# Layer one's bases of an R-GCN with the partition as (row, basis) and rows eight apart

## The chip, the core and the metric

The kernel runs on one core of one Trainium2 chip. The time is that of one execution on the device, in microseconds, as the median of several runs. A profiled execution is a separate run; its own device time and its span (first to last instruction) stand beside the median below.

## What is computed

Two blocks of a graph network over 625 nodes with 512 features. Each has a graph part, a linear attention and a mixture of experts. The change lies in the first graph part, a relational graph convolution with two relations, whose weights are mixed from 30 bases:

```python
def rgcn_gate_layer(x, row, col, edge_type, basis, att, gate_w, root, bias):
    w = jnp.einsum('rb,bio->rio', att, basis)      # basis (30, 512, 512), att (2, 30)
    x_j = x[col]
    msgs = []
    for r in range(2):
        gate = jax.nn.sigmoid(x_j @ gate_w[r, :, 0])
        msgs.append(gate[:, None] * x_j @ w[r])
    msg = jnp.where((edge_type == 0)[:, None], msgs[0], msgs[1])
    agg = jax.ops.segment_sum(msg, row, num_segments=x.shape[0])
    return agg + x @ root + bias

h = jax.nn.relu(rgcn_gate_layer(x, row, col, edge_type, basis1, att1, gate_w1, root1, bias1))
out = rgcn_gate_layer(h, row, col, edge_type, basis2, att2, gate_w2, root2, bias2)
```

Inputs and output are float32. The first line of the function is what matters here: for layer one, 30 x 512 rows of 2 KB, 31.5 MB, are read from HBM and summed into w[0] and w[1], 512 rows each.

## The kernel before

**Mixing layer one's bases** (`mix_bases_1`, lines 311 to 343) is done on PE in 32 steps q. A step takes 32 rows i of the weight (4 groups j of 8 neighbouring rows) and one half of the bases (15 of 30, g = q % 2). Its tile `basis` has 120 partitions, one for each pair (basis, row within the group), and four blocks j of 512 columns. Line 325 fills it with four loads on SP's queue, each of 15 bases x 8 rows x 512 values. Step q multiplies each block with `att1`, a matrix of 120 x 32 that holds att[r, b] where the partition's row is the column's row, and zero elsewhere (line 334). So 32 rows of PSUM get, in their first 16, the mixed rows (row, relation) of the group j; the second half of the bases is accumulated on the first. After every second step ACT copies the four groups to a tile `stage` (line 338), and POOL issues four small writes (line 341), each of which moves 16 rows of `stage` to 8 partitions of `wmix`, the weights as the messages need them: row i at partition i % 128 and column block i // 128.

`att1` is made once at the start (lines 436 to 452): `att_pick` repeats columns of the identity so that a matmul (line 444) brings att to the 120 partitions, `att_mask` (line 446) has a one where the partition's row is the column, and line 450 multiplies them.

**What runs beside it.** The stage that lasts until 185 us builds the matrix of edge counts: fifteen groups (`count_group`, lines 219 to 236) of one-hot rows made by DVE and ACT and multiplied on PE. Between groups, the loop of lines 536 to 552 places one or two mixing steps (`mix`), a piece of the linear attention, three or two additions of the first slice of layer two's weights (`slice0`, DVE, line 367) and the loads for it on POOL's queue (`ring`, line 356). The weights `wk`, `wv`, `wq` are loaded on SP's queue between the basis loads. The order of PE and SP is written out by hand here (`manual_schedule`), so both work through these calls in the order of the code. The tiles `basis` come from a pool with three buffers: a load waits until PE has used the tile before the last two.

**The last four steps** are threaded between layer two's other slices (`slices`, 30 loads of 768 KB into the same pool, added on DVE) in the order "DPDPDPDP" and then only D, lines 568 to 594, three loads ahead. Then `messages` (line 627) reads `wmix`: its first matmul needs every write of line 341.

Of the kernel before, what the change touches and what calls it, by code (L numbers as in the profile page):

```python
# [14 lines left out]
OP = mybir.AluOpType  # L15
AX = mybir.AxisListType
# [5 lines left out]
D = 512  # L22
# [4 lines left out]
NB = 30  # L27
BGROUPS = (15, 15)
BROWS = 8
# [16 lines left out]
def kernel(ctx: ExitStack, tc: tile.TileContext, A, out: bass.AP):  # L46
    nc = tc.nc
# [11 lines left out]
    ident = const.tile([128, 128], F32, name="ident")  # L59
# [111 lines left out]
    def one_bank():  # L171
        return banks[1].tile([128, BANK], F32, name="ps1")

    def mix_bank():
        return banks[2]()
# [135 lines left out]
    def mix_bases_1(wpool):  # L311

        w = wpool.tile([128, 2, KD * D], F32, name="wmix")
        src = A["L0_gnn_basis1"].rearrange("b (i c) o -> i b c o", c=BROWS)
        acc = [None]

        def loaded(q):  # L320
            i0, g = 4 * (q // 2), q % 2
            n, b0 = BGROUPS[g], sum(BGROUPS[:g])
            bt = basis_pool.tile([128, KD, D], F32, name="basis")
            for j in range(4):
                nc.sync.dma_start(bt[:BROWS * n, j, :], src[i0 + j, b0:b0 + n])
            return bt

        def step(q, bt):
            i0, g = 4 * (q // 2), q % 2
            k = BROWS * BGROUPS[g]  # L330
            if g == 0:
                acc[0] = mix_bank()
            for j in range(4):
                nc.tensor.matmul(acc[0][32 * j:32 * j + 32, :], att1[g][:k], bt[:k, j, :],  # L334
                                 start=(g == 0), stop=(g == 1))
            if g == 1:
                sg = stage_pool.tile([128, D], F32, name="stage")
                nc.scalar.copy(sg, acc[0])  # L338
                for j in range(4):
                    k, p0 = (i0 + j) // 16, 8 * ((i0 + j) % 16)  # L340
                    nc.gpsimd.dma_start(w[p0:p0 + 8, :, k * D:(k + 1) * D], sg[32 * j:32 * j + 16, :])  # L341

        return w, [(lambda q=q: loaded(q), lambda bt, q=q: step(q, bt)) for q in range(32)]

    class Added:
# [91 lines left out]
    b0 = 0  # L437
    for n in BGROUPS:
        k = BROWS * n
        pick = dec.tile([NB, 128], F32, tag="part", name="att_pick", bufs=3)  # L440
        nc.vector.tensor_copy(pick[:, :k].rearrange("p (b c) -> p b c", b=n),
                              ident[:NB, b0:b0 + n, None].to_broadcast([NB, n, BROWS]))
        ps = one_bank()
        nc.tensor.matmul(ps[:k, :2], pick[:, :k], attT, start=True, stop=True)
        mask = rowsA.tile([128, BROWS], F32, name="att_mask", bufs=2)
        nc.vector.tensor_reduce(mask[:k], ident[:k, :k].rearrange("p (b c) -> p c b", b=n), AX.X, OP.add)
        a = rowsA.tile([128, 32], F32, name=f"att1_{b0}")
        nc.gpsimd.memset(a, 0.0)
        for r in range(2):
            nc.vector.tensor_scalar_mul(a[:k, r:2 * BROWS:2], mask[:k], ps[:k, r:r + 1])  # L450
        att1.append(a)
        b0 += n
# [6 lines left out]
    for i in range(2):  # L459
        g = rowsA.tile([128, KD, 32], F32, name=f"gwp{i}")  # L460
# [46 lines left out]
    def gates_of(psg):  # L507
        gate = rowsA.tile([P, NT, 2], F32, name="gate")
        nc.scalar.activation(gate.rearrange("p t r -> p (t r)"), psg[:P, :2 * NT], AF.Sigmoid)
        return gate  # L510

    wm1, steps = mix_bases_1(wpool)

    def mix(n=1):
# [261 lines left out]
    pick = lpool.tile([P, NT], F32, name="pick")  # L776
# [804 lines left out]
```

## Time and profile before

| | us |
|---|---|
| median of 3 runs | 978.2 (977.06 to 979.41) |
| the profiled execution, device time | 975.78 |
| its span | 974.0 |
| PE busy | 890.9 (91%) |
| DVE busy | 514.2 (53%) |
| ACT busy | 304.1 (31%) |
| POOL busy | 142.8 (15%) |
| basis loads of line 325: first and last issue | 3.3 and 215.4 |
| one issue of line 325 on SP's queue (median of 128) | 0.838 |
| one mixing matmul of line 334 (256 in all), mean of the first 224, median of the last 32 | 0.650, 0.617 |
| writes of line 341: one issue on POOL, median landing | 0.550, 6.7 |

The profile divides the span into 40 equal slices and gives busy shares in tenths (a 9 is 90% or more), the clock granted to PE in tenths, and for the DMA engines the mean busy share of sixteen and the rate:

```profile
PE   3898899979999999789969999999988899997997
DVE  7778694566889723422254632233355754566320
PEclk9999999999999999799989999999999999997999
DMA  8899997575487920889831111212210104020001
GB/s 243 244 280 259 251 248 185 169 196 196 135 285 230 334 87 2 265 292 331 281 120 56 44 43 47 81 46 87 86 64 27 61 1 128 10 77 2 0 6 47
```

Each slice is 24.4 us. The count stage takes the first seven and a half. PE is busy nearly everywhere; the DMA engines are busy in the first half of the span and mostly idle in the second. A group of instructions is listed by line, engine, operation, output and inputs; "mean ns" is one instruction, and the idle time is that of its engine just before.

### The profile page before, as it was taken

Reading aid. Unit: us, or ns where it says so; the run is one execution under the profiler, and the core shown is the slowest. Engines: PE = TensorE matmul, PEld = TensorE weight load, DVE = VectorE, ACT = ScalarE, POOL = GpSimd, SP = SyncE. Lnnn points to the kernel's source line nnn. Section 1 sums busy time; section 2 is a strip of 40 time slices with the busy share of each in tenths; the row PEclk is TensorE's granted clock in tenths of the full one; section 3 lists DMA queues with packets and bytes.
Section 4 is the critical chain, followed back from the end, with each engine's and each line's share of the span. In section 5 each row is a group of like instructions: output and inputs, shape, how many; then the busy total and the mean of one; then the engine's idle time right before and its main releaser. Section 6 shows DMA issues by size and latency. Waiting matters only on the chain. (4 is left out here: it accounts for less than half of the span.)

```text
span 974.0 us, 10135 instructions
## 1 busy us (share of the span) xinstructions
PE 890.9 (91%) x3606; PEld 488.1 (50%) x3606; DVE 514.2 (53%) x980; ACT 304.1 (31%) x508; POOL 142.8 (15%) x223
## 2 busy tenths in 40 slices
PE   3898899979999999789969999999988899997997
PEld 1333234534474448767735655555544554444543
DVE  7778694566889723422254632233355754566320
ACT  2566475611120021111125432322243442311310
POOL 6644231110000200330020000000000000011310
PEclk9999999999999999799989999999999999997999
DMA  8899997575487920889831111212210104020001
GB/s 243 244 280 259 251 248 185 169 196 196 135 285 230 334 87 2 265 292 331 281 120 56 44 43 47 81 46 87 86 64 27 61 1 128 10 77 2 0 6 47
DMA packets 70842, 135.06 MB, mean 139 GB/s; under 512 B 9298, under 2 KB 11485, under 8 KB 70787
## 3 DMA queue, kind: packets, MB, share of 16 engines
q1 hardware_dynamic: 61554, 114.19, 38.3%
q0 software_dynamic: 9232, 20.16, 6.9%
q8 instruction: 31, 0.51, 0.2%
q14 instruction: 25, 0.20, 0.1%
HBM read 123.37 MB, written 8.85 MB: 136 GB/s over the span
## 5 line engine op out<-in xcount | busy, mean ns | idle before, releaser
L367 DVE SCALAR_TENSOR_TENSOR wmix<-basis,att,wmix 128x1536 f32<-128x1536 f32 x58 | 101.4, 1811 | 12.8 <-DMA basis<-in_L_gnn_basis_dram 12.8
L133 PE MATMUL ps<-y1T,wh 128*128 128x512 f32 (+1 forms) x256 | 74.5, 440 | 1.5 <-DVE hm L1281 1.0
L138 PE MATMUL ps<-hm,wh 128*128 128x512 f32 (+1 forms) x256 | 71.7, 433 | 0.0
L233 DVE TENSOR_SCALAR os<-iota,edges,wbits 125x626 bf16<-125x626 f16 x123 | 49.9, 469 | 26.6 <-PE tail L236 26.5
L138 PE MATMUL ps<-wmix,xnT 128*125 128x512 f32 x140 | 61.9, 592 | 0.0
L235 PE MATMUL main<-os,odg 125*128 125x512 bf16 x165 | 48.7, 381 | 11.9 <-ACT os L231 6.4
L133 PEld LDWEIGHTS ps<-y1T,wh 128*128 128x128 f32 x256 | 41.1, 190 | 33.8 <-issue 30.6
L138 PEld LDWEIGHTS ps<-hm,wh 128*128 128x128 f32 x256 | 39.7, 191 | 30.7 <-issue 30.7
L341 POOL DMA_DIRECT2D wmix<-stage x64 | 37.0, 581 | 98.2 <-ACT stage L338 98.1
L334 PE MATMUL mix<-basis,att 120*32 120x512 f32 x224 | 42.4, 650 | 8.8 <-DVE att L450 5.6
L659 PE MATMUL ps<-z,counts 125*125 125x512 f32 x200 | 48.3, 397 | 0.6 <-PEq L644 0.6
L1291 DVE TENSOR_TENSOR acc<-acc,sg 128x625 f32<-128x625 f32 x15 | 12.2, 811 | 64.1 <-ACT sg L1289 64.1
L367 DVE SCALAR_TENSOR_TENSOR w<-ring,att,w 128x512 f32<-128x512 f32 x58 | 40.8, 752 | 9.8 <-DMA ring<-in_L_gnn_basis_dram 9.8
L1281 DVE TENSOR_SCALAR hm<-ps,bh 128x625 f32<-128x625 f32 x32 | 27.7, 867 | 31.4 <-PE ps L133 31.4
L138 PEld LDWEIGHTS ps<-wmix,xnT 128*125 128x125 f32 x140 | 26.3, 188 | 33.8 <-issue 33.0
L1279 ACT ACTIVATE hm<-ps,bh 128x625 f32<-128x625 f32 x32 | 25.0, 782 | 55.4 <-PE ps L133 55.4
L138 PEld LDWEIGHTS ps<-xgT,w1e 128*128 128x128 f32 x320 | 38.1, 199 | 7.7 <-ACT xgT L1021 7.7
L659 PEld LDWEIGHTS ps<-z,counts 125*125 125x125 f32 x200 | 36.5, 185 | 10.8 <-issue 2.2
L138 PE MATMUL ps<-xgT,w1e 128*128 128x128 f32 x320 | 39.9, 285 | 1.2 <-ACT xgT L1021 1.2
L138 PE MATMUL ps<-w2e,hTe 128*128 128x512 f32 x80 | 37.5, 595 | 3.0 <-DVE hTe L1030 3.0
L636 ACT ACTIVATE z<-ps,gate 125x512 fp32r<-125x512 f32 x20 | 13.7, 687 | 79.9 <-PE ps L138 79.9
L133 PE MATMUL ps<-xnT,wq 128*128 128x113 f32 (+1 forms) x128 | 36.5, 438 | 2.0 <-DVE cT L74 1.2
(358 smaller groups left out, 1522.6 us busy)
## 6 DMA issues: line engine op xcount, KB each, us to landing
basis<-in_L_gnn_basis_dram SPq DMA_DIRECT2D x128, 240.0 KB
basis<-in_L_gnn_basis_dram SPq DMA_DIRECT2D x30, 768.0 KB
w1e<-in_L_ffn_W_dram SPq DMA_DIRECT2D x10, 1024.0 KB
w2e<-in_L_ffn_W_dram SPq DMA_DIRECT2D x10, 1024.0 KB
ring<-in_L_gnn_basis_dram POOLq DMA_DIRECT2D x30, 256.0 KB, 7.9
wh<-in_L_gnn_Wh_dram SPq DMA_DIRECT2D x4, 1024.0 KB
xd<-stage POOLq DMA_DIRECT2D x12, 256.0 KB, 6.4
b2row<-in_L_ffn_b_dram SPq DMA_DIRECT2D x10, 256.0 KB
```

Source lines behind the costliest of these rows:

```text
L133: nc.tensor.matmul(ps[:m, lo:hi], l, r[:, lo:hi], start=(i == 0), stop=(i == len(pairs) - 1))
L138: nc.tensor.matmul(ps, l, r, start=(i == 0), stop=(i == len(pairs) - 1))
L233: nc.vector.tensor_scalar(os_, iota, edges[:, 0, c:c + 1], wfield[:, c:c + 1], op0=OP.is_equal, op1=OP.mult)
L235: nc.tensor.matmul(main0, od[:, c - c0, :], os_[:, :BANK], start=c == 0, stop=c == NE - 1)
L334: nc.tensor.matmul(acc[0][32 * j:32 * j + 32, :], att1[g][:k], bt[:k, j, :], start=(g == 0), stop=(g == 1))
L341: nc.gpsimd.dma_start(w[p0:p0 + 8, :, k * D:(k + 1) * D], sg[32 * j:32 * j + 16, :])
L367: nc.vector.scalar_tensor_tensor(w[:, r, :], self.tiles[b], c, w[:, r, :], op0=OP.mult, op1=OP.add)
L636: nc.scalar.activation(hi[:, t, :], ps[:P], AF.Copy, scale=g)
L659: nc.tensor.matmul(ps[:P], l, r, start=first and i == 0, stop=last and i == len(pairs) - 1)
L1279: nc.scalar.activation(hm[:, m, :], ps[:, :N], AF.Relu, bias=b)
L1281: nc.vector.tensor_scalar(hm[:, m, :], ps[:, :N], b, 0.0, op0=OP.add, op1=OP.max)
L1291: nc.vector.tensor_add(acc, acc, sg)
```

## The change

Within a load, the order of the 120 pairs turns from (basis, row) to (row, basis), and the eight rows of a load are no longer neighbours but eight apart. One step still covers 32 rows and 15 bases with four loads of 240 KB, and there are still 128 loads. A load's source now has 8 rows (16 KB apart) outermost and 15 bases (1 MB apart) inside, where it had 15 bases outermost and 8 neighbouring rows (16 KB in one piece) inside. The tile's partitions are filled in order as before. Since the rows of a group are eight apart, a write of line 341 goes to eight partitions with a step of eight, where it went to eight neighbours. The two constant matrices are built for the new order.

```diff
         w = wpool.tile([128, 2, KD * D], F32, name="wmix")
-        src = A["L0_gnn_basis1"].rearrange("b (i c) o -> i b c o", c=BROWS)
+        src = A["L0_gnn_basis1"].rearrange("b (q c i) o -> q i c b o", c=BROWS, i=8)
         acc = [None]
 
         def loaded(q):
-            i0, g = 4 * (q // 2), q % 2
+            g = q % 2
             n, b0 = BGROUPS[g], sum(BGROUPS[:g])
             bt = basis_pool.tile([128, KD, D], F32, name="basis")
             for j in range(4):
-                nc.sync.dma_start(bt[:BROWS * n, j, :], src[i0 + j, b0:b0 + n])
+                nc.sync.dma_start(bt[:BROWS * n, j, :], src[q // 4, 4 * (q // 2 % 2) + j, :, b0:b0 + n])
             return bt
 
         def step(q, bt):
-            i0, g = 4 * (q // 2), q % 2
+            g = q % 2
             k = BROWS * BGROUPS[g]
...
                 nc.scalar.copy(sg, acc[0])
+                k, p0 = q // 8, 64 * (q // 4 % 2) + 4 * (q // 2 % 2)
                 for j in range(4):
-                    k, p0 = (i0 + j) // 16, 8 * ((i0 + j) % 16)
-                    nc.gpsimd.dma_start(w[p0:p0 + 8, :, k * D:(k + 1) * D], sg[32 * j:32 * j + 16, :])
+                    nc.gpsimd.dma_start(w[p0 + j:p0 + j + 57:8, :, k * D:(k + 1) * D], sg[32 * j:32 * j + 16, :])
...
-        nc.vector.tensor_copy(pick[:, :k].rearrange("p (b c) -> p b c", b=n),
-                              ident[:NB, b0:b0 + n, None].to_broadcast([NB, n, BROWS]))
+        nc.vector.tensor_copy(pick[:, :k].rearrange("p (c b) -> p c b", b=n),
+                              ident[:NB, None, b0:b0 + n].to_broadcast([NB, BROWS, n]))
...
-        nc.vector.tensor_reduce(mask[:k], ident[:k, :k].rearrange("p (b c) -> p c b", b=n), AX.X, OP.add)
+        nc.vector.tensor_reduce(mask[:k], ident[:k, :k].rearrange("p (c b) -> p c b", b=n), AX.X, OP.add)
```

## The prediction, made before the changed kernel was run

> **What bounds the kernel now.** I began with the chain of work that ended last. Its first piece starts at 494.57 us, so it says nothing of the stretch the change touches: layer one's bases are loaded and mixed between 3 and 221 us. For that stretch I cut the span into parts and read busy time by engine (columns: stretch, its length, then busy us and instruction count of PE, PEld, DVE, ACT and POOL, the granted clock, the mean busy share of the sixteen DMA engines, GB/s):
>
> ```profile
> 20.00:60.00 40.00, 34.27 (x176) 14.70 (x177) 30.62 (x53) 24.92 (x36) 26.23 (x38) 1.00 0.91 257
> 60.00:150.00 90.00, 80.39 (x384) 31.23 (x381) 74.66 (x132) 51.44 (x71) 29.80 (x55) 0.98 1.00 258
> 150.00:185.00 35.00, 34.24 (x225) 18.96 (x224) 18.62 (x49) 25.37 (x51) 2.17 (x4) 1.00 0.58 161
> 225.00:330.00 105.00, 104.26 (x353) 56.07 (x352) 93.48 (x61) 14.44 (x27) 0.00 (x0) 1.00 0.68 220
> ```
>
> From 60 to 150 us the DMA engines have no free time, at only 258 GB/s, and PE is 89% busy beside them. The DMA engines and PE bound this stage together, DMA slightly ahead. From 225 us PE is busy 99% of the time: what arrives late before that point moves everything behind it. The list of waits up to 190 us agrees (waiter, line, what it waited for: us in total, times, longest):
>
> ```profile
> PEld mix L334 <- DMA basis<-in_L_gnn_basis_dram: 15.9, 19, 2.7
> ...
> PE mix L334 <- DMA basis<-in_L_gnn_basis_dram: 3.1, 4, 1.8
> ```
>
> So PE already loses 19.0 us to these loads. The first 28 of 32 steps end at 185 us; the last four are threaded between layer two's slices until 221 us.
>
> Next, the DMA view of 0 to 185 us (queue: packets, MB, share of 16 engines):
>
> ```profile
> q1 hardware_dynamic: 18129, 32.83, 66.3%
> q0 software_dynamic: 4560, 10.77, 21.9%
> ```
>
> and the same line for 225 to 330 us, then for 420 to 460 us:
>
> ```profile
> q1 hardware_dynamic: 12042, 22.93, 67.2%
> ...
> q1 hardware_dynamic: 6440, 12.59, 87.8%
> ```
>
> Share times sixteen engines times length, divided by MB, is a price in engine-us per MB. In 0 to 185 us: 0.663 x 16 x 185 = 1962, over 32.83 = **59.8** (122 ns for a 2 KB packet). In 225 to 330 us (layer two's slices): 1129 / 22.93 = **49.2** (101 ns). In 420 to 460 us (expert weights): 562 / 12.59 = **44.6** (91 ns). All move runs of 2 KB, so layer one's loads are dear by their pattern.
>
> **The change: the loads.** There are still 128 loads of 240 KB, each of 120 runs of 2 KB; only their order turns from (15 bases, 8 rows) to (8 rows, 15 bases). That decides over how many DMA engines a load is spread. The trace's semaphore records show it for before: of the sixteen increments that complete a load of line 325, one arrives about 1.3 us after issue and the other fifteen, singly, some 4 us later. Loads with 128 partitions on both sides get all sixteen late; loads of 13 partitions get thirteen, of 125 only five, of 8 eight. The Trainium skill, DMA: Bandwidth & Descriptors, section on why a DMA increments its semaphore by 16, gives the rule: a transfer runs on the largest number of engines, up to 16, that divides the slowest dimension of both sides, on the sync queue the lowest-numbered ones; the sequencer adds the rest of the increments at once. Before: 15 and 120 give 15, as recorded. After: the source's slowest dimension is 8 and the tile has 120 partitions, so 8. The counts of this trace follow the rule for every shape, and it speaks against the change: the same bytes on **eight engines in place of fifteen**, and always the same eight. By the q1 row alone, spread as now, the sum would be no change; by the rule it is this:
>
> - Steps 1 to 28 load 112 x 0.2458 = 27.5 MB. At 59.8 that is 1646 engine-us, 110 us on each of fifteen engines. Everything else up to 185 us, (0.663 + 0.219 + 0.003) x 2960 - 1646 = 974 engine-us, lies on all sixteen: 61 us. Busy 171 of 185 us, idle 14.
> - After, the price must be chosen. Upper end 59.8: pattern costs stay. Lower end 44.6. I take 49.2, because in layer two's slices one engine also steps between distant rows while its neighbours read a few rows away, which is what rows eight apart make of layer one. The skill's same page (latency and other measured facts) lists a drop from 207 to 164 GB/s when the row pitch of concurrent streams goes from 512 KiB to 2 MiB; now the engines stand 1 MiB apart, afterwards 16 KB, so it too points down, though those were copies inside HBM and nothing here isolates it.
> - 27.5 x 49.2 / 8 = 169 us on each of the eight. The other traffic costs 61 us at its present price, 50 if it eases by 49.2/59.8: I take 56. Idle shrinks to about 5 us, the first issue being at 3.3 us and two tiles always queued. Sum 230 us where there were 185: **+45 us**. No cover: PE has 154 us of work in those 185, but it consumes the tiles in a written order, and each step is late.
>
> SP's issues (128 at 0.84 us) are as many and stay under the transfer time: four take 3.4 us, a tile's transfer 60 x 0.1 = 6 us. Behind a waiting issue SP holds wk, wv, wq, root and layer two's slices; their shift is in the sum. The POOL queue's ring loads share the eight engines with it and come somewhat later, then DVE's adds (line 367) and the one-hot rows behind them, which PE needs; a step is later still.
>
> **The last four steps** (185 to 221 us). PE waits there for the bases too:
>
> ```profile
> PEld ps L334 <- DMA basis<-in_L_gnn_basis_dram: 9.3, 7, 2.5
> ...
> PE ps L334 <- DMA basis<-in_L_gnn_basis_dram: 6.2, 5, 3.0
> ```
>
> One tile, 0.983 MB, takes 0.983 x 59.8 / 15 = 3.9 us now, 6.0 us on eight engines at 49.2, 7.3 at 59.8. The first was issued at 183 and used at 196.6 us, so it has cover; three have next to none: 3 x 2.1 to 3 x 3.4, I take **+8 us**.
>
> **The write-back and the set-up.** 64 POOL issues of 0.55 us as before, the same 16 rows of 2 KB, to partitions eight apart. Landing now takes 3.1 to 8.4 us, and only the last is waited for (0.2 us by PE at 229.9 us), with no slack left. The ends of that row bound it at -0.2 and +2 us (landing 6.7 becoming 8.4); nearest is no change: 0. The two copies (0.26 us) and two reductions (0.34 us) of the set-up keep their sizes and end at 9.8 us, before line 450 at 15.3 us, which stands behind the iota cast: 0, or a few tenths if that cover went.
>
> **Sum.** 45 + 8 = +53 us on the profiled execution: span 974.0 to 1027, its device time 975.8 to 1029. The median of the runs is 978.2, 2.4 above that execution, hence **1031 us**.
>
> **Rivals.** *The packets keep their price* (59.8). For it: even from 150 to 185 us, with hardly any POOL traffic, the price is 0.555 x 560 / 5.39 = 57.7. Then 27.5 x 59.8 / 8 = 206, and 206 + 61 + 5 = 272 us, +87, and +10 for the last four: 1075 us. *The packets fall to the expert weights' price* (44.6): 153 + 46 + 5 = 204 us, +19, and +6: 1003 us; against it, those loads meet almost no other pattern. *On the other side:* the load is spread as widely as before, because the 15 becomes the split or the rows are divided otherwise, and rows eight apart take the pattern's cost away. At 49.2 on fifteen engines the DMA work is 90 + 50 = 140 us, below PE's 154, and PE decides. It could win back at most 19.0 + 15.5 us; I take a third of it, as the order and DVE's one-hot rows hold it too: about 966 us. It decides from the number of engines k at which 1353 / k + 50 falls under 171, so from 12. Against it is every count in the records. *No change* would need price and spread to cancel.
>
> **How the numbers follow.** Forecast (about 1012 to 1050) 0.47; price kept 0.25; price at its floor 0.18; other side 0.06; cancelling, or some cover I have not seen, 0.04. A difference within 0.2%, about what runs of this kernel can tell from nothing, gets 0.03 of it; slower 0.91, faster 0.06. The range runs from just under the floor case to just over the kept price, 1000 to 1078 us.
>
> **What would show it.** In the changed profile: a completion of line 325 with eight late increments; the stage up to 28 steps ending near 230 us at a mean DMA share near 0.6, never 1.0, since eight engines are full and eight have little; PE's wait for basis loads growing from 19 to some 60 us; a q1 price near 49; everything after layer one's last step shifted unchanged. The prediction is wrong if fifteen or sixteen increments come late, if the DMA share stays at 1.0, or if the price goes to an end.

## The result and the profile after

The changed kernel takes 1009.5 us (median of 4 runs, 1008.68 to 1010.65) where the one before takes 978.81 (median of 4, 977.06 to 980.84): a ratio of **1.031 (95% interval 1.029 to 1.034)**, 30.7 us slower. Its profiled execution has a span of 1007.3 us against 974.0, that is +33.3; the working below uses these two executions.

PE, DVE, ACT and SP have the same instructions in the same order, and POOL too apart from one branch among its writes, so a mixing step can be set beside its counterpart. The end of the last matmul of a step (start of the last one, us from the span's start), read from the trace by time:

| step | before | after | later by |
|---|---|---|---|
| 2 | 19.4 | 26.3 | 7.0 |
| 6 | 43.0 | 52.3 | 9.3 |
| 12 | 82.5 | 98.9 | 16.4 |
| 18 | 118.0 | 145.6 | 27.6 |
| 21 | 135.2 | 164.9 | 29.7 |
| 28 | 185.6 | 215.3 | 29.7 |
| 32 | 221.2 | 254.5 | 33.3 |
| end of the span | 974.0 | 1007.3 | 33.3 |

The loss builds up from the second step to the twenty-first, a little is added in the last four, and from there the rest of the kernel is shifted unchanged. From step 21 to step 28 nothing is added: there both kernels take 7.2 us a step, and PE is busy for 48.3 of these 50.4 us in both.

The table of stretches for the changed kernel, in the columns of the prediction's first block:

```profile
20.00:60.00 40.00, 32.77 (x146) 12.88 (x148) 23.51 (x41) 18.52 (x26) 21.63 (x31) 0.96 0.62 207
60.00:150.00 90.00, 73.55 (x279) 24.08 (x277) 53.82 (x95) 40.01 (x55) 25.57 (x50) 0.96 0.68 212
150.00:185.00 35.00, 31.93 (x192) 13.89 (x194) 30.27 (x56) 22.89 (x35) 8.19 (x15) 1.00 0.65 214
185.00:215.00 30.00, 29.49 (x188) 16.71 (x184) 14.56 (x41) 20.75 (x44) 2.17 (x4) 1.00 0.55 170
```

Read the next to last column first. From 60 to 150 us the mean share of the sixteen DMA engines has dropped from 1.00 to 0.68 and the rate from 258 to 212 GB/s. That looks like relief; a reader of the mean alone would say that DMA no longer binds. But PE has become idler too (73.6 us busy in place of 80.4), and the list of waits up to 205 us says for what:

```profile
PEld mix L334 <- DMA basis<-in_L_gnn_basis_dram: 47.9, 33, 2.7
...
PE mix L334 <- DMA basis<-in_L_gnn_basis_dram: 19.5, 23, 1.8
```

The waits for layer one's bases went from 19.0 to 67.4 us. Not all of this is lost time, since a weight load (PEld) waits while matmuls run: up to the end of step 28 PE is idle for 41.9 us, where it was 30.9. A mean share of 0.68 with a queue that PE waits for suggests that some of the sixteen are full while others rest. The trace has the start and length of every DMA packet, and they show it: from 60 to 150 us there are never fewer than eight packets in flight, and eight or nine in 60% of the time, where the kernel before has 15 to 17 in 86%. From 150 to 200 us SP's queue alone has more than eight in flight in only 19% of the time, so the loads that are queued behind one another use the same eight. The semaphore records say how many engines one load has: each of the 128 loads of line 325 now shows one increment about 1.1 us after issue and **eight** late ones, where it showed fifteen.

The DMA view of the changed kernel, first from 0 to 205 us, then from 150 to 200 us, when nothing but layer one's bases is on SP's queue:

```profile
q1 hardware_dynamic: 16711, 31.58, 48.1%
q0 software_dynamic: 4560, 10.77, 18.3%
```

```profile
q1 hardware_dynamic: 3887, 7.46, 42.7%
```

By the prediction's rule (share x 16 x length / MB) the first line gives 0.481 x 3280 / 31.58 = 50.0 engine-us per MB, the last 0.427 x 800 / 7.46 = 45.8. The first mixes in wk, wv, wq and root; the last is the bases' own price in a stretch with less POOL traffic (57.7 before, from 150 to 185 us).

In the last four steps, the list of waits from 215 to 360 us:

```profile
PEld ps L334 <- DMA basis<-in_L_gnn_basis_dram: 14.8, 8, 2.9
PE ps L334 <- DMA basis<-in_L_gnn_basis_dram: 7.5, 7, 2.5
```

That is 22.3 us where there were 15.5.

### The profile page after: what moved, and what is told of

The parts are those of the page before. It is cut to its first block, busy times and chain, and to the rows that moved or that the text cites. A ratio compares the mean times of both kernels' runs of the same rounds, so it can differ in the third digit from the quotient of the medians.

```text
span 1007.3 us, 10135 instructions
## 1 busy us (share of the span) xinstructions
PE 910.9 (90%) x3606; PEld 488.2 (48%) x3606; DVE 512.2 (51%) x980; ACT 304.7 (30%) x508; POOL 141.8 (14%) x223
## 5 line engine op out<-in xcount | busy, mean ns | idle before, releaser
L334 PE MATMUL mix<-basis,att 120*32 120x512 f32 x224 | 61.1, 639 | 25.1 <-DMA basis<-in_L_gnn_basis_dram 19.5
L233 DVE TENSOR_SCALAR os<-iota,edges,wbits 125x626 bf16<-125x626 f16 x123 | 49.2, 464 | 60.5 <-PE tail L236 60.5
L138 PEld LDWEIGHTS ps<-hm,wh 128*128 128x128 f32 x256 | 39.7, 191 | 30.7 <-issue 30.7
L659 PE MATMUL ps<-z,counts 125*125 125x512 f32 x200 | 48.3, 397 | 0.6 <-PEq L644 0.6
L138 PEld LDWEIGHTS ps<-wmix,xnT 128*125 128x125 f32 x140 | 26.3, 188 | 33.8 <-issue 33.0
L334 PEld LDWEIGHTS mix<-basis,att 120*32 120x32 f32 x224 | 9.3, 110 | 63.3 <-DMA basis<-in_L_gnn_basis_dram 47.9
L138 PE MATMUL ps<-xgT,w1e 128*128 128x128 f32 x320 | 39.3, 282 | 0.7 <-ACT xgT L1021 0.7
```

The lines of the kernel that those rows point to most:

```text
L138: nc.tensor.matmul(ps, l, r, start=(i == 0), stop=(i == len(pairs) - 1))
L233: nc.vector.tensor_scalar(os_, iota, edges[:, 0, c:c + 1], wfield[:, c:c + 1], op0=OP.is_equal, op1=OP.mult)
L659: nc.tensor.matmul(ps[:P], l, r, start=first and i == 0, stop=last and i == len(pairs) - 1)
```

## The experiments

The theory is the rule that the prediction cites: a load runs on the largest number of engines, up to sixteen, that divides the slowest dimension of both its sides, and the change costs time because this number fell from fifteen to eight. The rivals: the spacing of the rows, the write to every eighth partition, or the order of the pairs as such (short pieces with jumps of 1 MB). A second question is what sets a packet's price. Each kernel was compared with the one before on the same chip, whose median lay between 975.5 and 979.3 us.

| run | layout of a load | late increments | median, us | ratio (95% interval) | price on SP's queue, 60 to 150 us |
|---|---|---|---|---|---|
| before | 15 bases, 8 rows | 15 | 978.8 | | 62.7 |
| after | 8 rows, 15 bases | 8 | 1009.5 | 1.031 (1.029 to 1.034) | 49.3 |
| e1 | 15 bases, 8 rows apart | 15 | 978.1 | 1.001 (0.999 to 1.003) | 63.4 |
| e2 | 8 neighbouring rows, 15 bases | 8 | 1019.6 | 1.040 (1.035 to 1.045) | 52.5 |
| e4 | 16 neighbouring rows, 8 or 7 bases | 16 | 978.2 | 1.002 (0.999 to 1.004) | 62.3 |
| e5 | 8 or 7 bases, 16 neighbouring rows | 8, 7 | 1027.0 | 1.050 (1.045 to 1.055) | 53.0 |
| e6 | 16 rows apart, 8 or 7 bases | 16 | 973.8 | 0.997 (0.995 to 0.999) | 61.5 |
| e7 | 4 rows, 30 bases | 4 | 1159.4 | 1.186 (1.181 to 1.190) | 45.7 |
| e9 | 30 bases, 4 rows | 15 | 989.6 | 1.012 (1.008 to 1.016) | 62.5 |
| e8 | 120 consecutive rows | 15 | 974.9 | 0.996 (0.995 to 0.998) | 60.4 |
| e12 | the same, one load a tile | 15 | 994.2 | 1.020 (1.016 to 1.023) | 71.8 |
| e10 | 15 bases, 8 x 4 rows, one load a tile | 15 | 999.4 | 1.024 (1.021 to 1.027) | 69.6 |
| e11 | 16 x 4 rows, 8 or 7 bases, one load a tile | 16 | 995.3 | 1.021 (1.017 to 1.024) | 65.1 |
| e13 | 128 consecutive rows | 16 | 960.1 | 0.981 (0.978 to 0.984) | 50.2 |

The price of a row is worked out from the DMA view of that run, as above (1440 engine-us in the stretch). It takes in the other loads of SP's queue.

### One half of the change each (e1, e2)

e1 keeps the rows eight apart and the strided write and puts the bases outermost again:

```diff
-        src = A["L0_gnn_basis1"].rearrange("b (q c i) o -> q i c b o", c=BROWS, i=8)
+        src = A["L0_gnn_basis1"].rearrange("b (q c i) o -> q i b c o", c=BROWS, i=8)
...
-                nc.sync.dma_start(bt[:BROWS * n, j, :], src[q // 4, 4 * (q // 2 % 2) + j, :, b0:b0 + n])
+                nc.sync.dma_start(bt[:BROWS * n, j, :], src[q // 4, 4 * (q // 2 % 2) + j, b0:b0 + n])
```

> One half of the change: rows eight apart and the write to every eighth partition stay, the order of the pairs goes back to (basis, row), so the source's slowest dimension is 15 again. Engine count (my theory): fifteen late increments per load, step 28 again near 185 us, median 975 to 985 us. Rival, the spacing of the rows or the strided write-back costs the time: 1000 to 1010 us although fifteen engines work.

e2 takes the kernel before and turns only the order:

```diff
-        src = A["L0_gnn_basis1"].rearrange("b (i c) o -> i b c o", c=BROWS)
+        src = A["L0_gnn_basis1"].rearrange("b (i c) o -> i c b o", c=BROWS)
...
-                nc.sync.dma_start(bt[:BROWS * n, j, :], src[i0 + j, b0:b0 + n])
+                nc.sync.dma_start(bt[:BROWS * n, j, :], src[i0 + j, :, b0:b0 + n])
```

> The other half: (row, basis) with neighbouring rows, contiguous write-back. Engine count: eight late increments, step 28 near 215 us, 1003 to 1016 us. Rival, spacing or write-back: 975 to 985 us. On the packet's price: if it fell from 59.8 to about 46 us per MB because fewer engines run at once, it is near 46 to 50 here too; if rows eight apart relieved the memory, it stays near 60 and the kernel is slower than the change, 1040 to 1075 us.

(In both, the two set-up matrices follow the order.) e1 has fifteen late increments and the time of before; e2 has eight and is slower, by 10 us more than the whole change and a little beyond the stated 1016. So the loss goes with the order, and the spacing and the strided write cost nothing. On eight engines rows eight apart are even worth some 6 us: e2's step 32 ends 6.0 us after that of the change (260.5 against 254.5 us). The other 4.4 us between the two profiled runs came later, and e2's have a lower granted clock over the span (0.966 against 0.974); its one run at 0.975 took 1014.86 us. On SP's queue from 60 to 150 us, e1 and then e2:

```profile
q1 hardware_dynamic: 8018, 14.69, 64.7%
```

```profile
q1 hardware_dynamic: 6735, 12.99, 47.4%
```

0.647 x 1440 / 14.69 = 63.4 and 0.474 x 1440 / 12.99 = 52.5: the price falls with the number of engines at work, although e2's rows are neighbours. That the spacing made packets cheap, as the prediction's argument for 49.2 had it, holds for a small part at most: on fifteen engines it did nothing, on eight it goes with 52.5 becoming 49.3.

### The same order with other counts (e4, e5, e6)

Is it the order or the count? With groups of 16 rows and 8, 8, 7 and 7 bases the two part: now (row, basis) divides by 16 and (basis, row) by 8 or 7.

```diff
-BGROUPS = (15, 15)
-BROWS = 8
+BGROUPS = (8, 8, 7, 7)
+BROWS = 16
...
-            i0, g = 4 * (q // 2), q % 2
+            i0, g = 4 * (q // 4), q % 4
...
-                                 start=(g == 0), stop=(g == 1))
-            if g == 1:
+                                 start=(g == 0), stop=(g == 3))
+            if g == 3:
...
-                    k, p0 = (i0 + j) // 16, 8 * ((i0 + j) % 16)
-                    nc.gpsimd.dma_start(w[p0:p0 + 8, :, k * D:(k + 1) * D], sg[32 * j:32 * j + 16, :])
+                    k, p0 = (i0 + j) // 8, 16 * ((i0 + j) % 8)
+                    nc.gpsimd.dma_start(w[p0:p0 + 16, :, k * D:(k + 1) * D], sg[32 * j:32 * j + 32, :])
```

e4 loads with `"b (i c) o -> i c b o"`, e5 with `"b (i c) o -> i b c o"`, e6 as e4 with the rows eight apart. The order of the instructions is the same in the three.

> Groups of 16 neighbouring rows and 8, 8, 7, 7 bases, (row, basis) as in the change: source and tile have 16 and 128 or 112 as slowest dimensions, so sixteen engines. Engine count: the DMA work up to step 28 is 27.5 MB x 50 to 60 / 16 + 50 to 61 = 136 to 164 us, so PE's 154 us decide: 958 to 975 us, faster than both. Rival, the (row, basis) order with its jumps of 1 MB costs the time: slower than before, 985 to 1010 us.

> The same groups of 16 neighbouring rows in the old order (basis, row): pieces of 32 KB, slowest dimension 8 or 7, so eight or seven engines. Engine count: slower than before although this is the old order, 1005 to 1030 us. Rival, the order (basis, row) with its long pieces is what makes before fast: 970 to 982 us.

> Groups of 16 rows, (row, basis), now with the rows eight apart: sixteen engines again. Engine count alone: as with neighbouring rows, 972 to 982 us. On the packet's price: rows eight apart were worth 10 us on eight engines (1009.5 against 1019.6); if they relieve the memory on sixteen too, the price falls from about 60 to 50 us per MB and the kernel is 960 to 972 us.

e5 decides: the old order is now the slow one, with eight and seven late increments, 48.8 us behind e4, which differs in nothing but the order. **It is the count and not the order.** (e5 never has fewer than seven packets in flight from 60 to 150 us.) e4 itself came out level with before and not faster, against what I expected. Two things bear on it. Its price stayed at 62.3, so sixteen engines in place of fifteen bring little. And it is level with before up to step 6, then loses 9.8 us at once; the list of waits of e4 from 38 to 64 us names the place:

```profile
PE main L235 <- DVE os L233: 8.7, 2, 8.4
DVE w L367 <- DMA ring<-in_L_gnn_basis_dram: 7.4, 1, 7.4
```

DVE stands 7.4 us before an addition of layer two's slice, whose ring load POOL had issued late among its own work, and the one-hot rows that PE needs are behind it. The order of the instructions on DVE and POOL differs from before in e4, which has fewer writes; whether that alone costs the 9.8 us was not tried. e6 has e4's order, only its rows are eight apart, and it does a little better: 0.997 (0.995 to 0.999). It is the only kernel of this study with the reference's weights that is faster than before, by 0.3%. Its price, 61.5, is not the 50 of the second expectation.

### The dose (e7, e9)

Groups of 4 rows and all 30 bases, with writes of 4 partitions; e7 with the rows outermost, e9 with the bases outermost, the same in all else:

```diff
-BGROUPS = (15, 15)
-BROWS = 8
+BGROUPS = (30,)
+BROWS = 4
...
-        src = A["L0_gnn_basis1"].rearrange("b (i c) o -> i b c o", c=BROWS)
+        src = A["L0_gnn_basis1"].rearrange("b (i c) o -> i c b o", c=BROWS)
```

> The dose: groups of 4 neighbouring rows and all 30 bases, (row, basis), slowest dimensions 4 and 120, so four engines; writes of 4 partitions, twice as many. Engine count: 27.5 MB x 45 / 4 + 51 + 5 = 365 us up to step 28, that is +180, and about +25 for the last four: 1150 to 1190 us, and the delay grows up to step 28 and doesn't stop at step 18. Rival, the order of the pairs costs a fixed sum per load: 1005 to 1030 us as with eight rows.

> The control of the dose: the same groups of 4 rows and 30 bases in the order (basis, row), slowest dimensions 30 and 120, so fifteen engines, pieces of 8 KB, the same doubled number of copies and writes. Engine count: 975 to 992 us. Rival, the small groups with their copies and writes cost the time: close to the run with four engines.

The two have the same instructions in the same order on every engine. Four engines take 1159.4 us, fifteen 989.6: 170 us by the count alone. The delay of e7 grows through all steps (step 18 ends at 226.5, step 28 at 350.9 us), and its price is the lowest. Its DMA view from 60 to 150 us (40 slices of 2.25 us, busy tenths and rate, and the line of SP's queue):

```profile
DMA  2222222222222894532222223872223422222225
GB/s 99 99 100 98 100 100 106 104 107 99 98 100 100 243 254 117 182 110 101 99 100 98 97 97 124 233 186 102 96 102 125 167 100 98 101 99 98 99 100 170
...
q1 hardware_dynamic: 4507, 8.94, 28.4%
```

0.284 x 1440 / 8.94 = 45.7, close to the floor of the prediction. Never fewer than four packets are in flight, and four or five in 80% of the time. In the slices with a 2 the bases run nearly alone, on four engines at some 98 to 100 GB/s: that is about 41 engine-us per MB (an estimate, 4 / 0.098). The sum of packet times gives more, because five or more packets at once count in full although four engines carry them. PE's granted clock in this stretch is 0.80 (0.98 before); with the four engines always at work it does not explain the delay. e9 is 1.2% behind before; it has twice the copies and writes, and which of them costs it was not tried.

### What makes a packet dear on fifteen engines (e8, e12, e13, e10, e11)

e8 takes the jumps of 1 MB away from the kernel before:

```diff
-        src = A["L0_gnn_basis1"].rearrange("b (i c) o -> i b c o", c=BROWS)
+        src = A["L0_gnn_basis1"].rearrange("b i o -> (b i) o")
...
-                nc.sync.dma_start(bt[:BROWS * n, j, :], src[i0 + j, b0:b0 + n])
+                p0 = BROWS * n * (4 * q + j)
+                nc.sync.dma_start(bt[:BROWS * n, j, :], src[p0:p0 + BROWS * n])
```

> The kernel before, but each load reads 120 consecutive rows (240 KB in one piece), so that the weights mixed are not the reference's; the count stays at fifteen. On the packet's price: if the 1 MB between the streams of the fifteen engines makes the packets dear, the price up to 150 us falls from about 60 to 45 to 50 us per MB, PE's waits for the bases nearly vanish and the kernel is 955 to 970 us. If it is the number of engines at work at once, or the tile's side, the price stays at 57 to 62 and the time at 974 to 982 us.

The price stayed at 60.4; the jumps of 1 MB alone are not it. The prices so far (45.7 at 30 packets for an engine and load, 49 to 53 at 15, 60 to 63 at 8) also fit a fixed cost for each load on each engine, and e12 tests that with one load a tile:

```diff
-                p0 = BROWS * n * (4 * q + j)
-                nc.sync.dma_start(bt[:BROWS * n, j, :], src[p0:p0 + BROWS * n])
+            k = BROWS * n
+            nc.sync.dma_start(bt[:k], src[4 * k * q:4 * k * q + 4 * k].rearrange("(j p) o -> p j o", p=k))
```

> As the run that reads 120 consecutive rows (the weights mixed are not the reference's), but one load of 960 KB for a tile in place of four of 240 KB: fifteen engines as before, packets of 2 KB as before, 32 packets for an engine in one load in place of 8. On the packet's price: if it holds a fixed cost of each load on each engine, it falls from about 60 to 45 to 49 us per MB and the kernel is 955 to 969 us; if it comes from the number of engines at work at once, it stays at 57 to 62 and the kernel at 970 to 979 us.

The time, 994.2 us, lies beyond both stated ranges, and the price rose with a quarter of the loads, which speaks against a fixed cost for each load. From 60 to 150 us, e8 and then e12:

```profile
q1 hardware_dynamic: 9024, 16.53, 69.3%
```

```profile
q1 hardware_dynamic: 7162, 14.23, 71.0%
```

0.693 x 1440 / 16.53 = 60.4 against 0.710 x 1440 / 14.23 = 71.8. The edit changes one thing more: within a load, a partition's four rows are now 120 rows (240 KB) apart, where a load of e8 had neighbours only. The two forms with the reference's weights do without that: a partition holds four neighbouring rows (8 KB). This is e10; e11 does the same for the order (row, basis) with 16 rows and 8, 8, 7 and 7 bases.

```diff
-        src = A["L0_gnn_basis1"].rearrange("b (i c) o -> i b c o", c=BROWS)
+        src = A["L0_gnn_basis1"].rearrange("b (q c j) o -> q b c (j o)", c=BROWS, j=4)
...
-            for j in range(4):
-                nc.sync.dma_start(bt[:BROWS * n, j, :], src[i0 + j, b0:b0 + n])
+            nc.sync.dma_start(bt[:BROWS * n].rearrange("p j o -> p (j o)"), src[q // 2, b0:b0 + n])
```

> A correct form of the same: the order (basis, row) of before on fifteen engines, but a partition holds four neighbouring rows (8 KB in one piece), so a tile is one load of 960 KB; the groups' rows are four apart. If loads are dear each by a fixed cost, 955 to 969 us, faster than both; if not, 972 to 984 us.

> The order (row, basis) of the change, with 16 rows and 8, 8, 7, 7 bases, so sixteen engines, and 8 KB pieces, one load for a tile. If loads are dear each by a fixed cost, 952 to 968 us, faster than both; if not, 968 to 982 us.

Both lost 2%, beyond their stated ranges too, and their prices rose (69.6 and 65.1). Their time says little about the bases, though: up to 215 us DVE waits 39.3 us (e10) and 27.5 us (e11) for the ring's loads where it waited 9.8, while the waits of the first 28 steps for the bases are 26.3 and 12.7 us where they were 19.0. The granted clock from 60 to 150 us is also lower in all three forms (0.84 to 0.89, 0.98 before); what it costs was not tried.

e13 changes e8 to 128 rows and 128 partitions:

```diff
-                p0 = BROWS * n * (4 * q + j)
-                nc.sync.dma_start(bt[:BROWS * n, j, :], src[p0:p0 + BROWS * n])
+                p0 = 128 * ((4 * q + j) % 120)
+                nc.sync.dma_start(bt[:, j, :], src[p0:p0 + 128])
```

> Four loads for a tile again, but each of 128 consecutive rows into 128 partitions, so sixteen engines (the matmuls still use 120 partitions, and the weights mixed are not the reference's; 7% more bytes). Consecutive rows on fifteen engines kept the price at about 60 us per MB, and 128 or 112 partitions with jumps of 1 MB as well; layer two's slices and the expert weights have both 128 partitions and consecutive rows. If it takes both to make packets cheap, the price falls to 45 to 50 here and the kernel is 955 to 970 us; if the stage itself (POOL's traffic beside it, small loads one behind the other) makes them dear, it stays at 57 to 62 and the kernel at 972 to 982 us.

```profile
q1 hardware_dynamic: 8988, 16.46, 57.4%
```

That is its DMA view from 60 to 150 us: 0.574 x 1440 / 16.46 = 50.2. With 7% more bytes the kernel takes 960.1 us, and the wait for these loads up to 190 us falls from 19.0 to 6.2 us. So packets on fifteen or sixteen engines are cheap when a load has consecutive rows and all 128 partitions at once; either alone (e8, e4) left them near 60. Whether the second is the tile's side or the sixteenth engine, or whether it counts that e13's loads start at multiples of 256 KB, these runs don't tell; why a packet is dear stays open. No kernel with the reference's weights was found that has both, since each load must bring several bases.

## Why the prediction was right, and by how much it was off

- **The cause.** Fifteen engines became eight. Shown: eight late increments, eight packets in flight, and e5 and e4, e7 and e9, two pairs that differ in the order alone: of each pair the one with fewer engines is slower, once in the old order and once in the new.
- **The sum.** The forecast was +53 us on the profiled execution; it is +33.3. The first 28 steps were to bring 45 and brought 29.7. The mis-sized term is the work of the eight engines: 169 + 56 = 225 us were forecast, and the last load of step 28 landed at 205.9 us. The price of the bases was taken as 49.2 and is 45.8 where they are alone on the queue, which makes 157 us; the rest of the packet time, (0.481 + 0.183 + 0.003) x 3280 - 27.5 x 45.8 = 928 engine-us, is 58 us on each of sixteen. These 215 us are still too many, since packets that overlap on an engine count twice. At e7's 41 engine-us per MB the bases need 141 us (an estimate); with the 58, and the 6.4 us in which fewer than eight packets are in flight, this makes 205. The rival with the expert weights' price, 1003 us, was nearer than my own case.
- **The idle time** was misread, and by luck this made up for part of the first error: of the 225 us at work about 199 were left, and the 5 us of idle time became 15.8 (6.4 + 9.4). In the kernel before, the last load of step 28 landed at 173.0 us and the step ended at 185.6: most of the 14 us that were booked as idle DMA time, to shrink to 5, is PE's own way behind the loads. It is 9.4 us now, since PE sets the pace from step 21 on, which the count of 28 equally late steps left out. So 32.9 us at the loads became 29.7 at the step.
- **Why 49.2.** The argument was the pattern: neighbours on rows apart. e1 and e2 show that the price came down mostly because fewer engines worked: of the way from 62.7 to 49.3, e2 has gone 10.2 with neighbouring rows, and the spacing adds 3.2. The bases alone are cheaper than layer two's slices (45.8 against 49.2). That 49.2 was near is luck in part. The Trainium skill's figures on row pitch (DMA: Bandwidth & Descriptors, latency and other measured facts), on which the argument leaned, got no support here: taking the 1 MB away changed the price from 62.7 to 60.4.
- **No cover from PE.** Nearly so. Up to the end of step 28 PE's idle time grew by 11.0 us, and the matmuls of line 334 keep it busy for 60.7 us where it was 42.0, with as many of them (220) at nearly the same mean (640 and 651 ns), so they overlap less. 11.0 + 18.7 is the whole delay. Only some 5 us of waits for DVE's one-hot rows (5.5 to 0.3) gave way. That PE already lost 19.0 us before was too much said for the same reason as above: 15.9 of them are waits of weight loads.
- **The last four steps.** +8 was taken, +3.6 came (33.3 - 29.7). A tile takes 5.6 us on eight engines at 45.8 and 5.0 at 41 (estimates), not 6.0; and of the three steps that were to have no cover, step 30 lost 1.5 and step 32 lost 2.1, but step 31 nothing.
- **Write-back and set-up at nothing.** Right: median landing 5.8 us (6.7 before), and PE waits for it 0.2 us as before; e1 confirms it with the strided write in place.
- **SP's issues.** Taken as equal; they became shorter, 0.670 us in place of 0.838, off the path.
- **The shift.** Right to the tenth: +33.3 at step 32 and at the end.
- **The signs named.** Eight increments, a mean share far from 1.0 (0.55 to 0.68), waits of some 60 us (67.4), a q1 price near 49 (50.0): all there. Only the end of step 28 was off (215.3 for 230). The rival on the other side needed twelve engines or more.

## What to carry to other kernels

Before turning the order of a load, write down the outermost size of both of its sides and count the engines; the mean share of the DMA engines hides the answer, since eight full ones and eight idle ones read as relief, while the waits of the consumer, the number of late increments and the number of packets in flight show it. Price a transfer from a stretch in which the same number of engines is at work and little else shares the queue, not from a queue's mean. A bigger load need not be a cheaper one: one of 960 KB in place of four of 240 KB made this kernel 2% slower than before in each of three forms.

## What the runs showed of the hardware that was not expected

- The same 2 KB packets, of several bases in a load, cost about 62 engine-us per MB on fifteen or sixteen engines and 45.7 to 53 on four to eight: halving the engines cost far less than half of the rate (from 60 to 150 us 258 against 212 GB/s for all queues, 174 against 150 for SP's).
- Consecutive rows on 120 partitions (60.4) and 128 or 112 partitions with jumps (62.3) are both dear; 128 consecutive rows on 128 partitions (50.2) are not.
- Fewer and larger loads went with a higher price per MB: 60.4 to 71.8 (e8 to e12, rows also read in another order), 62.7 to 69.6 (before to e10, packets of 8 KB).
- An issue on SP's queue takes 0.670 us (median) for a load on eight engines and 0.838 us for one of the same 120 runs on fifteen. The count alone does not set it: 120 consecutive rows on fifteen take 0.351 us (e8), and on four engines it is 2.5 us (e7).
